# Layer-0 input transposes of a two-layer graph-attention and mixture-of-experts kernel: by a second, block-swapped load and VectorE in place of TensorE

## The chip, the cores and the metric

The kernel runs on one core of a Trainium2 chip. The metric is the device time of one execution in microseconds (us). The core has five engines with a queue of instructions each: TensorE (PE: matmuls and transposes; its weight loads are shown apart as PEld), VectorE (DVE), ScalarE (ACT), GpSimd (POOL) and SyncE (SP), which only issues transfers. An engine works through its queue in order; where an instruction needs another engine's result it waits, and all behind it wait too. Transfers run on 16 DMA engines.

## The reference, cut to what matters

64 batches of 256 rows with 256 columns, all float32, go through two layers. Each line below adds to its own input (a residual).

```python
x = x + elu(attention4(layernorm(x), adj, W0, a0))     # 4 heads of 64, masked softmax over 256 rows
x = x + layernorm(x) @ Wf.T + bf
x = x + relu(attention1(layernorm(x), adj, W1, a1))    # 1 head of 256
x = x + moe(layernorm(x))                              # router, the 2 best of 8 experts, gelu
```

The expert layer also adds its normalised input, as `moe` starts from its tokens. The change touches the first line only: there the kernel needs the projection `layernorm(x) @ W0` (with the score columns), and for TensorE the rows of x must lie transposed, columns on the partitions.

## The kernel before, in words

A batch is a tile of 128 partitions with two row tiles of 256 columns (`[P, NT, D]`). `load_batch` fetches it three batches ahead (`AHEAD`, six buffers). `batch_layers` (from line 370) is a generator that carries one batch through both layers. A hand-written schedule (from line 896) runs it: a step calls every active generator once, in the order of the ranks that they yield, and a new batch begins every third step (`TICKS`). So several batches are in work at a time, each some stages behind the next, and the order of instructions on every engine is fixed when the program is built. Routing work (`route`), done once per chunk of up to four batches, and the experts' work on pairs of 128 rows (`expert_pair`) are woven in by the same steps.

The stages that matter here:

- Line 375, `norm_stats(x0)`: VectorE takes mean and variance of the rows (lines 290 and 291), GpSimd turns the variance into 1/std, called `rstd` (lines 293 and 294). The mean is taken out through the weights, and `rstd` is applied after the projection, so the projection itself works on raw x.
- Line 376, `transposed(x0)`: four 128x128 transposes on TensorE into a PSUM bank (`pt`, line 301), and one ScalarE copy to SBUF (`xT`, line 305). The same helper is used three more times per batch, for x1, x2 and the normalised rows `xng`.
- Line 378, `projected`: the matmuls `pq<-wx,xT` of line 315, 268 wide in layer 0 and 259 in layer 1, then the exponentials on ScalarE (line 323) and the scaling on VectorE (line 327), which need `rstd`.
- `scores` (lines 339 and 346) and `attended` (matmuls `pv`, line 360; reciprocals, line 367), then hp, e, x1 (lines 388 to 398).
- The second transpose, the dense layer `pf` (line 408), then layer 1 in the same way, then router, sending of rows to the experts' regions (line 741), expert matmuls `ph` (649) and `py` (664), and scatters that add into the output (line 681), each of which waits for earlier ones.

SBUF tiles come from pools with a fixed number of buffers per name (`bufs`); a tile whose buffer is still being read makes its writer wait. `work` has two buffers unless a call says otherwise; `xT` has four, and they are shared by all the transposed tiles.

## Time and profile before

| | |
|---|---|
| time, median of 3 runs | 1795.14 us (1784.11 to 1803.95) |
| span of the profiled execution | 1821.2 us |
| mean granted TensorE clock | 0.937 of full |
| busy: PE, PEld, DVE, ACT, POOL | 89, 79, 68, 46, 60% of the span |
| DMA packets | 137,374, of them 18,680 under 512 B; 192.90 MB |
| DMA queue of SyncE (q1), of GpSimd (q0) | 22.0%, 20.6% of 16 engines |
| last layer-0 transpose starts at | 1450.2 us |

How to read the lines of a profile below. A group line gives the source line, the engine, the operation, the tiles it writes and reads (out<-in), their shapes and the number of instructions; behind the first bar the busy time in us and the mean length of one in ns; behind the second bar the idle time of the engine just before them, and what ended it. A timeline line gives the start in us, the length, and the same names; square brackets hold the idle time before it and its releaser. A line of busy time by stretch gives from:to, length, the busy time of PE, PEld, DVE, ACT and POOL with the number of instructions, then the granted clock, the DMA share and the GB/s. PE's matmuls are pipelined, so the distance from one start to the next says what a group costs the engine.

### The profile page before, as it was taken

What the parts mean: (1) busy time and instruction counts of PE and PEld (TensorE: products, weight loads), DVE (VectorE), ACT (ScalarE), POOL (GpSimd) and SP (SyncE); (2) the same over time, 40 slices, a digit from 0 to 9 for tenths busy, and PEclk for the clock granted to TensorE, in tenths of its full rate; (3) what the DMA queues carried; (4) which work ended last, traced back from release to release, by engine and by line L of the source; (5) the groups of instructions that cost most, each with busy time, mean ns of one, the idle gap of its engine ahead of it and who ended that gap; (6) DMA issues with size and microseconds to landing.
All of it is one profiled execution on the core that took longest, in us unless ns stands there. A gap on an engine that the chain in (4) does not pass through costs nothing. (4 is left out here: it accounts for less than half of the span.)

```text
span 1821.2 us, 30155 instructions
## 1 busy us (share of the span) xinstructions
PE 1629.5 (89%) x9254; PEld 1433.0 (79%) x9254; DVE 1231.4 (68%) x4680; ACT 839.9 (46%) x1773; POOL 1084.2 (60%) x1164
## 2 busy tenths in 40 slices
PE   6998889899999999999999999999989998778692
PEld 5787778788888888888878788887878887667582
DVE  6889887867685858686766768688678876522231
ACT  1243333355554555554545545555455545443241
POOL 1333645557575767767676757576685767644444
PEclk9999989899998999998989999999899989889897
DMA  4410211235344444544354534444353436576663
GB/s 137 140 36 24 71 60 53 79 109 121 105 95 104 109 126 108 132 103 110 93 119 112 119 91 95 118 111 128 84 127 101 107 82 166 118 186 139 135 139 43
DMA packets 137374, 192.90 MB, mean 106 GB/s; under 512 B 18680, under 2 KB 91392, under 8 KB 137216
## 3 DMA queue, kind: packets, MB, share of 16 engines
q1 hardware_dynamic: 86592, 122.61, 22.0%
q0 software_dynamic: 49632, 67.39, 20.6%
q8 instruction: 76, 1.25, 0.3%
q10 hardware_dynamic: 992, 0.99, 0.2%
q14 instruction: 82, 0.67, 0.1%
HBM read 101.77 MB, written 89.15 MB: 105 GB/s over the span
## 5 line engine op out<-in xcount | busy, mean ns | idle before, releaser
L681 POOL DMA_INDIRECT out_dram<-y,to x262 | 419.4, 1601 | 231.1 <-DMA out_dram<-y,to 103.5
L360 PE MATMUL pv<-q,z 128*128 128x65 f32 (+1 forms) x2560 | 394.4, 314 | 5.3 <-DVE z L346 5.0
L360 PEld LDWEIGHTS pv<-q,z 128*128 128x128 f32 x2560 | 364.9, 210 | 21.1 <-DVE z L346 5.4
L293 POOL TENSOR_SCALAR rstd<-mv 128x2 f32<-128x2 f32 x256 | 81.2, 317 | 376.2 <-DVE mv L291 355.6
L741 POOL DMA_INDIRECT xs<-xng,pos x248 | 261.2, 1053 | 68.2 <-issue 66.0
L315 PE MATMUL pq<-wx,xT 128*128 128x268 f32 (+1 forms) x1024 | 265.4, 402 | 35.8 <-ACT xT L305 31.8
L649 PE MATMUL ph<-sT,we 128*128 128x256 f32 x1048 | 252.6, 397 | 48.1 <-ACT sT L621 22.9
L346 DVE SCALAR_TENSOR_TENSOR z<-pd,q,mask 128x256 f32<-128x256 f32 x640 | 265.1, 473 | 9.9 <-PE pd L339 7.5
L649 PEld LDWEIGHTS ph<-sT,we 128*128 128x128 f32 x1048 | 205.0, 200 | 80.6 <-ACT sT L621 29.4
L664 PE MATMUL py<-w2s,hT 128*128 (+1 forms) x1176 | 265.4, 381 | 0.6 <-ACT hT L655 0.6
L315 PEld LDWEIGHTS pq<-wx,xT 128*128 128x128 f32 x1024 | 188.1, 194 | 85.8 <-ACT xT L305 50.6
L664 PEld LDWEIGHTS py<-w2s,hT 128*128 128x128 f32 x1176 | 220.5, 191 | 29.3 <-ACT hT L655 1.0
L305 ACT COPY xT<-pt 128x512 f32<-128x512 f32 x256 | 144.9, 589 | 192.8 <-PE pt L301 127.6
L327 DVE SCALAR_TENSOR_TENSOR q<-pq,rstd,q 128x256 f32<-128x256 f32 x256 | 112.4, 479 | 154.5 <-ACT q L323 150.7
L655 ACT ACTIVATE hT<-ph,we 128x256 f32<-128x256 f32 x294 | 123.3, 471 | 173.4 <-PE ph L649 122.9
L670 DVE TENSOR_TENSOR y<-py,b2s 128x512 f32<-128x512 f32 x147 | 96.7, 688 | 149.2 <-PE py L664 77.9
L294 POOL TENSOR_TENSOR rstd<-rstd,mhalf 128x2 f32<-128x2 f32 x256 | 184.2, 719 | 21.4
L642 ACT ACTIVATE y<-y,w 128x256 f32<-128x256 f32 x262 | 112.9, 498 | 177.5 <-DVE y L670 171.1
L290 DVE BATCH_NORM_STATS2 stats<-x 128x6 f32<-128x256 f32 x384 | 155.9, 406 | 0.0
L408 PE MATMUL pf<-wfT,xT 128*128 128x256 f32 x512 | 145.7, 435 | 0.1
L323 ACT ACTIVATE q<-pq,rstd 128x12 f32<-128x12 f32 (+1 forms) x256 | 56.5, 265 | 162.3 <-POOL rstd L294 150.8
L434 POOL TENSOR_TENSOR x<-x,rel 128x512 f32<-128x512 f32 x64 | 109.2, 1706 | 25.2 <-ACT rel L431 25.0
(147 smaller groups left out, 2259.2 us busy)
## 6 DMA issues: line engine op xcount, KB each, us to landing
we<-wpack SPq DMA_DIRECT2D x147, 288.0 KB
xr<-xs SPq DMA_DIRECT2D x131, 260.0 KB
xin<-in_x_dram SPq DMA_DIRECT2D x64, 256.0 KB
out_dram<-base SPq DMA_DIRECT2D x64, 256.0 KB
out_dram<-y,to POOLq DMA_INDIRECT x262
xs<-xng,pos POOLq DMA_INDIRECT x248
xs<-fill SPq DMA_DIRECT2D x9, 260.0 KB
wpack<-wt SPq DMA_DIRECT2D x8, 288.0 KB
```

The source lines that it names most:

```text
L290: nc.vector.bn_stats(stats[:, t, :], src[:, t, :])
L294: nc.gpsimd.tensor_tensor(rstd, rstd, mhalf, ALU.pow)
L305: nc.scalar.copy(dst, pt)
L315: nc.tensor.matmul(pq.rearrange("p h c -> p (h c)"), xT[:, k, t * P : (t + 1) * P], wx[:, k, :], start=(k == 0), stop=(k == KT - 1),)
L346: nc.vector.scalar_tensor_tensor(z[:, j, :], pd[:, i, :], q[:, j, h, d + 2 : d + 3], mask[:, j, :], op0=ALU.max, op1=ALU.mult,)
L360: nc.tensor.matmul(pv[:, h, :], z[:, j, t * P : (t + 1) * P], q[:, j, h, : d + 1], start=(j == 0), stop=(j == NT - 1),)
L408: nc.tensor.matmul(pf[:, t, :], xT[:, k, t * P : (t + 1) * P], wfT[:, k, :], start=(k == 0), stop=(k == KT - 1),)
L649: nc.tensor.matmul(ph[:, f, :], we[:, k * D + f * P : k * D + (f + 1) * P], xT[:, k, :], start=(k == 0), stop=(k == KT - 1),)
L655: nc.scalar.activation(hT[:, f, :], ph[:, f, :], AF.Gelu, bias=we[:, C_B1 + f : C_B1 + f + 1])
L664: nc.tensor.matmul(py[:, t, :], hT[:, f, t * P : (t + 1) * P], w2s[:, e, f * D : (f + 1) * D].rearrange("p e c -> p (e c)"), start=(f == 0 ...
L681: d = nc.gpsimd.indirect_dma_start(out=out_rows, out_offset=bass.IndirectOffsetOnAxis(ap=to[:, t : t + 1], axis=0), in_=y[:, t, :], in_off ...
L741: d = nc.gpsimd.indirect_dma_start(out=xs_d[: E * CAP * PAIR, :], out_offset=bass.IndirectOffsetOnAxis(ap=at, axis=0), in_=xe, in_offset=None,
```

## The change

The raw rows of a batch are loaded a second time, as `xblk`. Four transfers per batch, each for 32 partitions, place every 32x32 block of the batch where its transpose belongs; the runs are 32 floats long. VectorE's `transpose` then turns all the 32x32 blocks in place of their own, in one instruction of 128x512, which gives the whole transposed tile `xT`. TensorE's four transposes and ScalarE's copy for layer 0 are no longer there; the other three transposes of a batch stay as they were. The block tiles are loaded two batches ahead into three buffers. To make room in SBUF, the tiles e, x1b and rel go from two buffers to one. What it is for: to take work off TensorE.

```diff
+    def load_blocks(b):
+        t = io.tile([P, KT, N], F32, tag="xblk", name=f"xblk_{b}", bufs=3)
+        for g in range(P // S):
+            nc.sync.dma_start(
+                out=t[g * S : (g + 1) * S].rearrange("q k (c a) -> q k c a", a=S),
+                in_=x[b].rearrange("(c q) (k g a) -> g q k c a", q=S, g=P // S, a=S)[g],
+            )
+        return t
+
+    S = 32
+    AHEAD, BLOCKS_AHEAD = 3, 2
+    xblk = {0: load_blocks(0)}
     xin = {0: load_batch(0)}
...
+    xblk.update({b: load_blocks(b) for b in range(1, BLOCKS_AHEAD)})
     xin.update({b: load_batch(b) for b in range(1, AHEAD)})
...
         _, rstd = norm_stats(x0)
-        xT = transposed(x0)
+        xb = xblk.pop(b)
+        if b + BLOCKS_AHEAD < B:
+            xblk[b + BLOCKS_AHEAD] = load_blocks(b + BLOCKS_AHEAD)
+        xT = work.tile([P, KT, N], F32, tag="xT", name="xT", bufs=4)
+        nc.vector.transpose(xT.rearrange("p k n -> p (k n)"), xb.rearrange("p k n -> p (k n)"))
         yield 20
...
-        ex = work.tile([P, NT, D], F32, tag="e", name="e")
+        ex = work.tile([P, NT, D], F32, tag="e", name="e", bufs=1)
...
-        x1b = work.tile([P, NT, D], F32, tag="x1b", name="x1b")
+        x1b = work.tile([P, NT, D], F32, tag="x1b", name="x1b", bufs=1)
...
-        rel = work.tile([P, NT, D], F32, tag="rel", name="rel")
+        rel = work.tile([P, NT, D], F32, tag="rel", name="rel", bufs=1)
```

## The prediction

> **What bounds the kernel now.** I read the page's first part, the groups by shape, the waits, the busy time by stretch, and the timeline of two batches.

> ```profile
> PE 1629.5 (89%) x9254; PEld 1433.0 (79%) x9254; DVE 1231.4 (68%) x4680; ACT 839.9 (46%) x1773; POOL 1084.2 (60%) x1164
> ```

> TensorE (PE) is the bound. By stretch (us; then busy time of PE, PE's weight loads, VectorE, ScalarE, GpSimd; clock; DMA share; GB/s):

> ```profile
> 60.00:300.00 240.00, 217.86 (x1304) 189.76 (x1303) 199.59 (x690) 84.45 (x200) 107.41 (x156) 0.94 0.18 57
> 300.00:900.00 600.00, 569.75 (x3355) 505.90 (x3354) 435.46 (x1619) 313.32 (x652) 399.91 (x433) 0.96 0.43 107
> ```

> PE is 91 to 95% busy, but VectorE (DVE) is 83% busy before 300 us and 73% after: it has room in sum, not everywhere. The groups of the work that moves, and the nearest DVE row:

> ```profile
> L305 ACT COPY xT<-pt 128x512 f32<-128x512 f32 x256 | 144.9, 589 | 192.8 <-PE pt L301 127.6 <-PE pl L475 42.4 <-remote 12.2
> ...
> L397 DVE SCALAR_TENSOR_TENSOR x<-hp,xin 128x512 f32<-128x512 f32 x64 | 43.9, 685 | 0.0
> ...
> L301 PE MATMUL pt<-ident,xin 128*128 128x128 f32 x256 | 39.8, 280 | 0.0
> ```

> A share says nothing about order, so the deciding view is the timeline (start, length, engine, line). One early batch:

> ```profile
> 112.25 0.60 PE L301 MATMUL pt<-ident,xin 128*128 128x128 f32 x4
> ...
> 112.69 0.38 PE L339 MATMUL pd<-ident,q 128*128 128x128 f32 x2
> ...
> 113.63 2.07 PE L315 MATMUL pq<-wx,xT 128*128 128x268 f32 x8 [0.56 <-ACT xT L305]
> ...
> 115.36 0.18 DVE L291 BATCH_NORM_AGGREGATE mv<-stats 128x2 f32<-128x6 f32 x1
> 115.46 0.85 DVE L346 SCALAR_TENSOR_TENSOR z<-pd,q,mask 128x256 f32<-128x256 f32 x2
> ...
> 115.98 3.68 PE L360 MATMUL pv<-q,z 128*128 128x65 f32 x32
> ...
> 119.70 0.18 DVE L367 RECIPROCAL rinv<-pv 128x4 f32<-128x4 f32 x1 [1.60 <-PE pv L360]
> ```

> PE runs the layer-0 projection (pq, 268 wide) at 113.63, while DVE finishes the statistics of the same rows only at 115.5. DVE runs about 2 us behind PE here, and nobody minds, because the projection needs xT and not the statistics.

> What an idle PE costs beyond the idle time shows at 1044 us:

> ```profile
> 1044.43 1.09 PE L617 MATMUL px<-ident,xr 128*128 128x128 f32 x4 [2.53 <-DMA xr<-xs]
> 1045.31 6.93 PE L360 MATMUL pv<-q,z 128*128 128x65 f32 x32
> 1052.04 3.00 PE L408 MATMUL pf<-wfT,xT 128*128 128x256 f32 x8
> ```

> After a gap of 2.53 us the same 32 matmuls take 6.93 us and not 3.68, and the next eight 3.00 and not 1.95 (their usual length in this stage): 4.3 us more. Shorter gaps, such as the 0.56 above, are followed by normal lengths.

> [...]

> **The change, part by part.**

> Removed from PE: four transposes of xin per batch. By start to start (112.25 to 112.69) they take 0.44 us, so 64 x 0.44 = 28 us. The 0.56 wait for ScalarE's copy goes too. Removed from ScalarE: 64 copies x 0.589 = 38 us, at 46% busy and off the path: worth nothing by itself.

> Added to DVE: 64 transposes of 128x512 f32. Below: as fast as the 685 ns row of that size. [...] I take 0.75 with its start, 48 us in sum. That DVE has room for.

> Moved: who makes xT. In the changed program's instruction order the transpose stands on DVE right behind the statistics of the same rows, and the projection on PE, unmoved in PE's order, now waits for DVE. This is the step that decides. In the batch above DVE could begin at 115.46 and end at 116.2. PE, without its four transposes and the copy's wait, is there at 113.07 - 0.44 = 112.6. A gap of 3.6 us takes the place of one of 0.56, and the projection starts 2.6 us later than before. Queued behind it on PE are xng's transposes, the experts' transposes px and the 32 attention matmuls (pv); for those DVE's rinv already waits (1.60). So DVE's next round starts later as well, it has hardly a gap from 119.70 to the next statistics, and the delay isn't caught up. The gap is also over 2.5 us, so the slow clock is due: up to 4.3 more. That is 6.9 us for a plain early batch of 15.7. Where routing work lies on DVE (batches 9, 10, 13, 14, 17, 18) the lag in the trace is 5 to 11 us, but the second of each pair has part of it paid by the first, and present PE waits (3.41 us for x at 163.5) fall away. I take 5.5 as the mean over the 19 batches before 350 us: 105 us.

> From there on, with two experts per batch on PE, the lag repeats in groups of four batches, about 100 us. One of the four, in the timeline:

> ```profile
> 1017.72 1.97 PE L315 MATMUL pq<-wx,xT 128*128 128x268 f32 x8
> ...
> 1020.76 0.18 DVE L291 BATCH_NORM_AGGREGATE mv<-stats 128x2 f32<-128x6 f32 x1
> ```

> With 0.75 us behind the statistics, xT would come, against the present start of the projection: 1.5 us early (the batch at 972 us), 1.0 late (995), 4.0 late (the one shown), 2.6 late (1038). With the 0.44 saved, gaps of 0, 1.4, 4.4 and about 2. The 4.4 costs the slow clock as well, 4.3. Given back: the wait for xr near 1041 to 1044 (3.1 in three pieces), whose own slow stretch now belongs to the gap before it, and 4 x 0.44 = 1.8. So 1.4 + 4.4 + 4.3 + 2 - 3.1 - 1.8 = 7. DVE's own waits in the group (2.65 and 4.94 us for ScalarE's q) take up some: I take 4 per group, 11 groups, 44 us.

> Added DMA: 64 x 4 transfers, each 512 runs of 128 B: 131,072 packets beside 137,374, 16.8 MB beside 193. Price per packet: below 14 ns (down from the 18 of 256 B), above 74 ns, the mean of queue q1 (22.0% of 16 x 1821.2 us over 86,592). At 16 ns it is 131 us per engine, 7% of the span on top of 43%: hidden, as a batch's blocks are asked for two batches ahead (30 us or more) and take some 2 us (10 at the upper price). Issue: a 512-run weight load costs SyncE 0.62 us, so 2.5 us per batch, in a queue that stands waiting 545 us for sent rows alone (its waits). At the start the first block load goes ahead of xin and the weights: +2 us.

> Cut buffers (e, x1b, rel from two to one): in the early batches x1b is read by 106.7 and rewritten at 113.1, e read by 110.8 and rewritten at 120.6, rel longer still. Nothing.

> Tail after the last projection (1454 us): same work, but the scatters, which wait 103.5 us on one another, get more time before it: -10.

> Sum: 105 + 44 + 2 - 10 = +141 us, with the 28 already taken off inside: 1795 + 141 = 1936.

> **Rivals.**
> *Waits without the clock (1850).* Gaps stay below what drops the clock, or DVE, freed by PE's pauses, catches up. Then only net delays remain: about 2.6 in half of the early batches (25) and 2 to 3 per group (30): +55. For it: DVE's idle 27% after 300 us. Against: DVE waits on PE's pv 91 times, so it cannot run ahead.
> *Hidden (1767, the other side).* xT is ready in time and the 28 us are pure gain. For it: PE at 95%, ScalarE relieved, one batch in four with xT early. Against: the statistics ahead of the transpose end after the projection's present start in three of four.
> *Packets (2065).* At 74 ns, DMA goes from 43 to 76%; the scatter chain (103.5 us of waits) and xr loads stretch by about 130 on top of 1936. Against: 18 ns for 256 B.

> **How the numbers follow.** Chances: 0.60 for 1936, 0.20 for 1850, 0.10 for 1767, 0.10 for 2065. The range leaves out the last two and takes in 1850 with 20 below it[...]: 1830 to 2010. Faster by over 1% 0.10; within 1% 0.04, from the low end of the second case; slower 0.86.

> **What would show it.** Right: projection matmuls waiting on the DVE transpose, some 100 to 200 us in over 40 waits; pv matmuls of double length behind them; a lower granted clock, most before 350 us; PE's busy share down; no DVE wait for xblk. Wrong: pq without idle, or DVE waiting for xblk, or scatters with longer landings. What would break the forecast most: a clock that doesn't drop, or a transpose far from 0.75 us.

## The result, and the profile after

| | before | changed |
|---|---|---|
| time, median | 1797.05 us (4 runs, 1784.11 to 1803.95) | 1928.24 us (4 runs, 1926.26 to 1936.97) |
| ratio to before | | 1.0748, 95% interval 1.0679 to 1.0818 |
| mean granted TensorE clock, profiled execution | 0.937 | 0.928 |

The changed kernel is 131 us slower, where 141 was forecast (1936), and the time lies in the range. One caution for all that follows: single executions of the kernel before spread over some 25 us, and its profiled one (span 1821.2) lies at the slow end, so the text compares spacings of batches and medians, not the two spans.

The same views as before, in the same order. The page's first part:

```profile
PE 1595.1 (83%) x8998; PEld 1397.3 (73%) x8998; DVE 1278.9 (66%) x4744; ACT 809.3 (42%) x1709; POOL 1081.5 (56%) x1164
```

TensorE has 256 transposes fewer (8998 instructions instead of 9254), and its share fell from 89 to 83%: it is busy for 34 us less (1595.1, 1629.5 before) while the time grew by 131, so it idles more than it saves. VectorE has 64 instructions more, 47.5 us, and its share fell too. So neither engine is held by the amount of its own work; something makes both wait. By stretch (PE, PEld, DVE, ACT, POOL, then clock, DMA share, GB/s):

```profile
60.00:300.00 240.00, 174.68 (x1005) 150.58 (x1004) 167.62 (x545) 61.09 (x144) 77.86 (x117) 0.87 0.26 66
300.00:900.00 600.00, 518.21 (x3070) 458.40 (x3069) 436.46 (x1584) 274.37 (x574) 365.70 (x408) 0.95 0.44 106
```

Before 300 us TensorE did 1005 matmuls where the kernel before did 1304, and its clock fell from 0.94 to 0.87. Who made it wait is in the chief group of the projection and in the list of waits (us in total, times, longest):

```profile
L329 PE MATMUL pq<-wx,xT 128*128 128x268 f32 (+1 forms) x1024 | 311.7, 455 | 220.5 <-DVE xT L394 197.8
```

```profile
PE pq L329 <- DVE xT L394: 197.8, 53, 11.9
```

The idle time ahead of the projections was 35.8 us before, nearly all of it for ScalarE's copy. It is 220.5 now, and 197.8 of that is waiting for VectorE's transpose, in 53 of 64 batches. The mean length grew from 402 to 455 ns as well, all of it in layer 0: the 128x268 matmuls go from 411 to 516 ns, the 128x259 ones stay at 394. Of the 512 in layer 0, 198 ran at a granted clock of 0.50, 667 ns each on the mean, against 407 for the 281 at full clock; in the kernel before 26 ran at 0.50. The transposed tile itself:

```profile
L105 SPq DMA_DIRECT2D xblk<-in_x_dram x256: 578/623/1748, 0.8 to 1504.6; - x128
L394 DVE STREAM_TRANSPOSE xT<-xblk x64: 692/711/714, 13.5 to 1559.2; 128x512 f32<-128x512 f32 x64
its engine sat idle before it (us, times) until:
who waited for it (us, times):
  PE pq L329: 197.8, 53
```

A transpose takes 711 ns, and VectorE never sat idle ahead of one: the list under "until" is empty. So the blocks were there each time, and no transfer stands behind the wait. VectorE was still busy with what its order puts first. An early batch shows it:

```profile
130.60 0.41 PE L353 MATMUL pd<-ident,q 128*128 128x128 f32 x2
...
133.71 0.18 DVE L305 BATCH_NORM_AGGREGATE mv<-stats 128x2 f32<-128x6 f32 x1
...
133.89 0.71 DVE L394 STREAM_TRANSPOSE xT<-xblk 128x512 f32<-128x512 f32 x1
...
134.65 2.07 PE L329 MATMUL pq<-wx,xT 128*128 128x268 f32 x8 [3.64 <-DVE xT L394]
...
137.00 3.68 PE L374 MATMUL pv<-q,z 128*128 128x65 f32 x32
...
140.72 0.18 DVE L381 RECIPROCAL rinv<-pv 128x4 f32<-128x4 f32 x1 [1.60 <-PE pv L374]
```

VectorE works without a break through the statistics of other batches' rows, then of these, then turns the blocks. TensorE stands for 3.64 us, and then VectorE stands 1.60 us for TensorE's pv, just as before: neither can get ahead of the other. Later, TensorE's own rows in one group of four batches:

```profile
1011.90 0.38 PE L353 MATMUL pd<-ident,q 128*128 128x128 f32 x2
1016.46 3.62 PE L329 MATMUL pq<-wx,xT 128*128 128x268 f32 x8 [4.18 <-DVE xT L394]
...
1020.93 3.69 PE L374 MATMUL pv<-q,z 128*128 128x65 f32 x32
...
1036.33 0.38 PE L353 MATMUL pd<-ident,q 128*128 128x128 f32 x2
1038.89 2.07 PE L329 MATMUL pq<-wx,xT 128*128 128x268 f32 x8 [2.18 <-DVE xT L394]
...
1041.24 1.48 PE L635 MATMUL px<-ident,xr 128*128 128x128 f32 x12
```

After the gap of 4.18 us the eight projection matmuls take 3.62 us and not 2.07, and pv behind them runs at full speed again. After 2.18 us nothing is slow. The wait of px for xr that the kernel before had here is gone: the gaps ahead of the projections have paid for it.

### The profile page after: what moved, and what is told of

Same layout as the page of the kernel before. It is cut to its first block, busy times and chain, and to the rows that moved or that the text cites. A ratio compares the mean times of both kernels' runs of the same rounds, so it can differ in the third digit from the quotient of the medians.

```text
span 1926.7 us, 29984 instructions
## 1 busy us (share of the span) xinstructions
PE 1595.1 (83%) x8998; PEld 1397.3 (73%) x8998; DVE 1278.9 (66%) x4744; ACT 809.3 (42%) x1709; POOL 1081.5 (56%) x1164
## 5 line engine op out<-in xcount | busy, mean ns | idle before, releaser
L329 PE MATMUL pq<-wx,xT 128*128 128x268 f32 (+1 forms) x1024 | 311.7, 455 | 220.5 <-DVE xT L394 197.8
L329 PEld LDWEIGHTS pq<-wx,xT 128*128 128x128 f32 x1024 | 213.0, 219 | 285.8 <-DVE xT L394 194.4
L374 PE MATMUL pv<-q,z 128*128 128x65 f32 (+1 forms) x2560 | 363.9, 298 | 0.0
L374 PEld LDWEIGHTS pv<-q,z 128*128 128x128 f32 x2560 | 337.8, 196 | 13.9
L667 PE MATMUL ph<-sT,we 128*128 128x256 f32 x1048 | 250.3, 395 | 43.9 <-ACT sT L639 24.0
L360 DVE SCALAR_TENSOR_TENSOR z<-pd,q,mask 128x256 f32<-128x256 f32 x640 | 264.6, 471 | 10.1 <-PE pd L353 10.1
L319 ACT COPY xT<-pt 128x512 f32<-128x512 f32 x192 | 112.3, 585 | 182.5 <-PE pt L315 181.4
L381 DVE RECIPROCAL rinv<-pv 128x4 f32<-128x4 f32 (+1 forms) x256 | 40.2, 170 | 193.9 <-PE pv L374 193.7
L412 ACT ACTIVATE e<-hp 128x512 f32<-128x512 f32 x64 | 40.3, 630 | 218.1 <-DVE hp L406 218.1
```

What stands on the lines that cost most here:

```text
L329: nc.tensor.matmul(pq.rearrange("p h c -> p (h c)"), xT[:, k, t * P : (t + 1) * P], wx[:, k, :], start=(k == 0), stop=(k == KT - 1),)
L360: nc.vector.scalar_tensor_tensor(z[:, j, :], pd[:, i, :], q[:, j, h, d + 2 : d + 3], mask[:, j, :], op0=ALU.max, op1=ALU.mult,)
L374: nc.tensor.matmul(pv[:, h, :], z[:, j, t * P : (t + 1) * P], q[:, j, h, : d + 1], start=(j == 0), stop=(j == NT - 1),)
L667: nc.tensor.matmul(ph[:, f, :], we[:, k * D + f * P : k * D + (f + 1) * P], xT[:, k, :], start=(k == 0), stop=(k == KT - 1),)
```

## The experiments

The theory is that the place of the transpose in VectorE's order costs the time. Rivals are the transfers and their packets, VectorE's extra work as such, the cut buffers, and a clock that falls by itself. Spacings below are from one start of a layer-0 projection to the next.

### Both made: all of the change but who makes xT

```diff
-        xT = work.tile([P, KT, N], F32, tag="xT", name="xT", bufs=4)
-        nc.vector.transpose(xT.rearrange("p k n -> p (k n)"), xb.rearrange("p k n -> p (k n)"))
+        turned = work.tile([P, KT, N], F32, tag="turned", name="turned", bufs=1)
+        nc.vector.transpose(turned.rearrange("p k n -> p (k n)"), xb.rearrange("p k n -> p (k n)"))
+        xT = transposed(x0)
```

> The changed kernel, with its block loads, its VectorE transposes and its cut buffers, but the transposes go into a tile that nobody reads, and TensorE and ScalarE make xT as before. If the loss is the wait of the projection for VectorE: near the kernel before, 1797 to 1815 us (the start still loads more). If it is VectorE's added load, the small packets or the cut buffers: 1920 to 1950, as in the changed kernel or above it.

Measured: 1796.65 us, ratio 1.0028 (1.0007 to 1.0049). The loads, the small packets, 64 more VectorE instructions in the very same place and the cut buffers cost together 0.3%, some 5 us (0.07 to 0.5% by the interval). The early stretch is as it was, with a DMA share of 0.32 where the kernel before had 0.18:

```profile
60.00:300.00 240.00, 217.42 (x1314) 189.66 (x1313) 210.38 (x708) 85.22 (x202) 108.66 (x157) 0.94 0.32 80
```

So it isn't the work that VectorE was given. It is that somebody waits for it.

### Copy on VectorE: only the lag, with nothing else of the change

The kernel before, with the copy of layer 0's transposes out of PSUM made by VectorE instead of ScalarE. TensorE still transposes; there are no block loads.

```diff
-        xT = transposed(x0)
+        xT = transposed(x0, copy=nc.vector.tensor_copy)
```

> The kernel before, and only the copy of the layer-0 transposes out of PSUM goes from ScalarE to VectorE, right behind the statistics: no block loads, no cut buffers, TensorE's transposes stay. If the wait for VectorE's place in the order is the cause: about as slow as the changed kernel, 1890 to 1960 us. If packets or buffers are: 1797 to 1810.

Measured: 1929.06 us, ratio 1.0748 (1.0712 to 1.0785): as much as the whole change, from handing one copy per batch to another engine. The waits:

```profile
PE pq L315 <- DVE xT L305: 177.1, 55, 12.2
```

TensorE keeps its 28 us of transposes here, but it does them where it would otherwise stand idle: the gap of a plain early batch is 3.10 us and not 3.65. Together the two runs show the cause from both sides: everything except the dependence costs 0.3%, and the dependence alone costs as much as the change.

### Ahead of the statistics: the same transpose, four instructions earlier

```diff
-        _, rstd = norm_stats(x0)
...
         nc.vector.transpose(xT.rearrange("p k n -> p (k n)"), xb.rearrange("p k n -> p (k n)"))
+        _, rstd = norm_stats(x0)
```

> The changed kernel, with the VectorE transpose ahead of the statistics of the same rows and not behind them, some 1.1 us earlier on VectorE. If the lag of VectorE is the cause, each of the 53 waits shrinks by about 1.1 us and the time falls by 50 to 60, to 1865 to 1885 us. If load, packets or buffers are: no change, 1920 to 1935.

Measured: 1865.9 us, ratio 1.0418 (1.0373 to 1.0463), 62 us less than the change. Each kind of gap shrank by 1.05 us (3.65 to 2.60, 4.18 to 3.13, 2.18 to 1.13, 1.17 to 0.12), about what the two pairs of statistics last (133.89 less 132.75 = 1.14 in the early batch above). The waits fell by 52.8 us in total; the other 9 were not measured apart, and the granted clock rose from 0.928 to 0.934.

```profile
PE pq L329 <- DVE xT L393: 145.0, 42, 10.8
```

What is left of the wait is the work of other batches that still stands ahead on VectorE.

### A batch earlier: the lag taken away

VectorE turns the blocks of the next batch while this one starts, behind its statistics, so each transpose has a whole batch of time. The transposed tile has two buffers of its own, and the shared xT three instead of four.

```diff
+        if b == 0:
+            turn(0)
         _, rstd = norm_stats(x0)
+        if b + 1 < B:
+            turn(b + 1)
+        xT = xT0.pop(b)
```

> The changed kernel, with the VectorE transpose of batch b + 1 issued at the start of batch b, so one batch earlier, into a tile of its own with two buffers (the shared xT goes from four to three). Work and transfers are the same. If the lag is the cause: the waits are gone, and what was taken off TensorE shows: 1765 to 1795 us. If load, packets or buffers are: 1910 to 1935.

Measured: 1803.8 us, ratio 1.004 (1.0018 to 1.0062). The wait for VectorE's transpose is gone from the list, and with it the loss. But 28 us of TensorE work are gone too, and of those nothing shows in the time. A miss, and the most useful one. Early on something does show: from the second projection to the 20th it is 314.8 us, where the kernel before took 324.7. But the second projection starts 9.7 us later (34.45 against 24.71), which takes it all back. Later the chief wait is another:

```profile
PE px L645 <- DMA xr<-xs: 29.3, 30, 2.7
```

In the timeline of a group of four:

```profile
447.49 0.63 PE L645 MATMUL px<-ident,xr 128*128 128x128 f32 x4 [2.09 <-DMA xr<-xs]
449.21 2.23 PE L645 MATMUL px<-ident,xr 128*128 128x128 f32 x8 [1.09 <-DMA xr<-xs]
451.23 6.93 PE L374 MATMUL pv<-q,z 128*128 128x65 f32 x32
457.95 3.72 PE L436 MATMUL pf<-wfT,xT 128*128 128x256 f32 x8
```

TensorE comes sooner to px, and the experts' rows aren't there yet. Behind these waits of 2.09 and 1.09 us pv takes 6.93 us and not 3.68, and pf 3.72 and not 1.95.

### Fill the wait: the clock's share by itself

The changed kernel with 28 transposes that nobody reads in the gap ahead of the projection, in the first 20 batches and in the one batch of each later four that has the 4.2 us gap: 31 in all. They are extra work, and keep TensorE busy for some 3 us (an estimate: 28 quarters of the 0.44 us of four transposes in the kernel before).

```diff
+        if b < 20 or b % 4 == 2:
+            idle = bank("idle", [P])
+            for _ in range(28):
+                nc.tensor.transpose(idle, x0[:, 0, :P], ident)
         q = projected(xT, wx0, H, rstd)
```

> The changed kernel, with 28 extra 128x128 transposes on TensorE, into a bank that nobody reads, right ahead of the projection in the batches that wait longest (the first 20, and of each later four the one that waits 4.2 us). They take 3.1 us of a wait that is there anyway. If the slow clock behind a wait costs 1 to 2 us each time, as the changed kernel's trace has it: 30 waits, so 1890 to 1905 us. If it costs nothing: 1925 to 1935. If it cost the 4.3 us of the prediction: 1830 to 1860.

Measured: 1903.11 us, ratio 1.0559 (1.0492 to 1.0626): 25 us less than the change by the medians, 34 by the two ratios to before (0.0189 of 1797), so 0.8 to 1.1 per filled gap and not 4.3. The early clock is whole again, and the mean of the profiled execution is 0.951, as in the kernel before on the same chip (0.936 to 0.951):

```profile
60.00:300.00 240.00, 206.33 (x1384) 183.65 (x1384) 178.75 (x589) 64.28 (x153) 85.61 (x126) 0.95 0.28 72
```

The spacing of the plain batches (us, from batch 4 to batch 8) splits the early loss cleanly:

| | spacing, mean of four | more than before |
|---|---|---|
| before, and "both made" | 15.4 | |
| changed, wait filled | 18.2 | 2.8 |
| changed | 20.0 | 4.6 |

So a plain early batch loses 2.8 us by waiting and 1.8 by the clock. The price per gap is a net one. In the six early batches with routing work gaps of 3.7 to 8.9 us remain. And in five of the later groups the slow stretch has moved to the next gap, the one of 2.18 us that cost nothing at 1038.89 above. The same batch here:

```profile
1017.64 3.76 PE L329 MATMUL pq<-wx,xT 128*128 128x268 f32 x8 [2.18 <-DVE xT L394]
```

### Three attempts to collect the 28 us, and what they met

*A mended start.* "A batch earlier", with the first three batches transposed by TensorE and the block loads behind the weights.

```diff
-    xblk = {0: load_blocks(0)}
+    FIRST = 3
+    xblk = {}
...
+        xT = xT0.pop(b) if b >= FIRST else transposed(x0)
```

> The kernel with the transpose a batch earlier, but the first three batches are transposed by TensorE as before, and the first block loads are issued behind the weights. If the block loads at the front are what puts its first projection 9 us late: 1792 to 1798 us, 6 to 10 below it and level with the kernel before. If not: 1800 to 1806.

Measured: 1814.25 us, ratio 1.0063 (1.0037 to 1.009). A miss; the two intervals overlap, so the mended start is neither shown better nor worse. The second projection starts at 31.3 us instead of 34.4, but the kernel before has it at 24.7: the block loads at the front are only about 3 of those 10 us. The traces show a second cause in the start. The tile e, cut to one buffer, is also the one into which the attention vectors of both layers are loaded when the weights are prepared (wx_a). The two loads in the kernel before (first and last start at the end of the line), then in the mended start, and VectorE's wait there:

```profile
L154 ACTq DMA_DIRECT2D wx_a<-in_L_gnn_a_dram x2: 453/488/522, 1.3 to 1.9; - x2
...
L168 ACTq DMA_DIRECT2D wx_a<-in_L_gnn_a_dram x2: 341/428/516, 1.3 to 11.7; - x2
...
  DMA wx_a<-in_L_gnn_a_dram: 3.2, 1
```

With one buffer layer 1's load waits until layer 0's vectors have been read. It starts at 11.7 us and not at 1.9 (15.5 in the changed kernel), and VectorE stands 3.2 us for it. How much of the late start it makes was not measured apart. Further on, more groups fall into the wait for xr with a slow stretch behind it (pv takes over 4.5 us in 7 batches between 350 and 1190 us, against 5 in the trace of "a batch earlier"), such as this one:

```profile
1031.26 0.63 PE L646 MATMUL px<-ident,xr 128*128 128x128 f32 x4 [2.26 <-DMA xr<-xs]
...
1034.82 6.93 PE L374 MATMUL pv<-q,z 128*128 128x65 f32 x32
```

*Pairs two steps later.* The mended start, and also the kernel before, with the experts' pairs begun two steps later, so that their rows have more time.

```diff
         if n:
+            if not last:
+                yield 95
+                yield 95
             regs = {}
```

> The same with the start mended, and expert pairs of a chunk become due two steps after its rows are sent (not for the last chunk), so that TensorE does not reach a pair's transposes before its rows are in. If the work taken off TensorE is lost in that wait and the slow clock behind it: 1740 to 1775 us. If it isn't: 1790 to 1805, or more by what is moved into the tail.

> The kernel before with the pairs two steps later and nothing else, the control of the one above. If the wait for a pair's rows costs this kernel its 3 us and the slow clock in each group of four batches: 1750 to 1780 us, and above the other by up to 28, what TensorE is spared. If not: 1795 to 1810.

Measured: 1899.1 us (ratio 1.053, 1.046 to 1.06) and 1879.34 us (1.038, 1.0279 to 1.0481). Both lie 124 and 99 us above the range of the theory, and above the rival's figures too. In the second, 30 us are lost by the last projection (1484.2 us, 1454.0 in the profiled execution of before, itself a long one), and 22 more from there to the end (388.9, 367.2). TensorE has new waits for VectorE, and the wait for xr has only shrunk, from 25.4 us:

```profile
PE pv L360 <- DVE y L670: 22.8, 13, 2.1
PE pt L301 <- DVE z L346: 18.3, 10, 2.1
PE px L617 <- DMA xr<-xs: 16.7, 14, 3.0
```

Two steps move whole stages of the pairs against everything else, into new waits and into the tail, where the wait asked for 3 us. What share each has was not measured apart.

*One rank later, not two steps.* The last attempt moves px only behind the attention matmuls pv of the same step, 3.7 us of work, by one rank, once on "a batch earlier" and once on the kernel before.

```diff
-        yield 40
+        yield 55
         px = bank("px", [KT, PAIR])
```

> The block transpose a batch earlier, as in the run of that name, and the experts' transposes px placed behind the layer-0 attention matmuls pv of the same step, not ahead of them. Theory (the 28 us saved on TensorE turned into a wait of px for the loaded rows xr, and the wait into slow matmuls): pv fills the wait, px waits under 0.5 us per group of four, no pv of double length at 450 or 645 us, 1755 to 1785. Rival (something else than xr holds the rate, such as VectorE): the waits move to pv or to the projections, 1795 to 1815.

> The kernel before, with px behind pv in the same way. Theory: its wait for xr of 2 to 3 us per group and the slow stretch behind it go too, 1765 to 1785, about 15 above the other run, as the 28 us on TensorE can then show in part. Rival: no better than before, 1790 to 1810, and no difference between the two runs.

Measured: 1764.87 us (ratio 0.9844, 0.9773 to 0.9915) and 1763.09 us (0.9834, 0.9763 to 0.9904). Both beat the kernels before and after, though the second was expected some 15 us above the first. The wait for xr fell to 3.6 us in the first and 7.7 in the second, and pv takes its 3.7 us in every batch from 350 to 1190 us. But the two are equal, so the 28 us still don't show. One part is the start again: the first kernel's second projection comes 9.75 us later (34.80 against 25.05), and by the 21st it has only about made that up (370.2 against 369.1). For the rest, the same place in both timelines tells why. First "a batch earlier" with px later:

```profile
627.01 3.69 PE L374 MATMUL pv<-q,z 128*128 128x65 f32 x32
630.53 1.48 PE L645 MATMUL px<-ident,xr 128*128 128x128 f32 x12
634.35 3.35 PE L436 MATMUL pf<-wfT,xT 128*128 128x256 f32 x8 [2.34 <-DVE q L341]
637.50 0.97 PE L353 MATMUL pd<-ident,q 128*128 128x128 f32 x4
```

and the kernel before with px later:

```profile
626.31 3.68 PE L360 MATMUL pv<-q,z 128*128 128x65 f32 x32
629.83 1.48 PE L617 MATMUL px<-ident,xr 128*128 128x128 f32 x12
632.82 1.99 PE L408 MATMUL pf<-wfT,xT 128*128 128x256 f32 x8 [1.51 <-DVE q L327]
634.65 0.60 PE L339 MATMUL pd<-ident,q 128*128 128x128 f32 x4
```

The wait is for q, and it goes back past VectorE, which stands idle itself. In the first kernel:

```profile
633.51 0.43 ACT L337 ACTIVATE q<-pq,rstd 128x12 f32<-128x12 f32 x2 [3.86 <-POOL rstd L308]
633.81 0.88 DVE L341 SCALAR_TENSOR_TENSOR q<-pq,rstd,q 128x256 f32<-128x256 f32 x2 [4.33 <-ACT q L337]
```

and in the second:

```profile
631.97 0.43 ACT L323 ACTIVATE q<-pq,rstd 128x12 f32<-128x12 f32 x2 [4.46 <-POOL rstd L294]
632.28 0.88 DVE L327 SCALAR_TENSOR_TENSOR q<-pq,rstd,q 128x256 f32<-128x256 f32 x2 [4.93 <-ACT q L323]
```

VectorE waits for ScalarE, and ScalarE for GpSimd's rstd. GpSimd goes through the same series of work in both, from the first sending of rows (xs) to that rstd in 13.5 us. TensorE, with less to do, reaches pv 0.83 us sooner in that series, and so waits that much longer: the gap grows from 1.51 to 2.34 us. With that the matmuls behind it slow down, and pf and pd take 1.7 us more. That is 2.5 us against the 1.76 saved by four batches without transposes. Between 350 and 1190 us the granted clock falls seven times, for 3.41 us each, in the first kernel and not once in the second. The spacing of a group agrees: 94.59 us with the change, 94.08 without (mean of seven groups, batches 24 to 52). The mended start together with the later px was not run.

## Why the prediction was right, and which terms were off

**The step that decides** (xT comes from VectorE, behind the statistics of the same rows, and the unmoved projection waits): right, and shown. The gap of a plain early batch was to be 3.6 us and is 3.65; those of a group of four were to be 0, 1.4, 4.4 and about 2, and are 0, 1.17, 4.18 and 2.18; the waits were to be 100 to 200 us in over 40, and are 197.8 in 53. In the six batches with routing they are 6.74 to 11.87 us; VectorE's place in the trace of before, with 0.75 us added, gives 6.8 to 12.0 for the same batches. All of it comes from comparing where VectorE stood with where TensorE needed the result. One discount failed: the second of each pair was to have part of its lag paid by the first, but its gap is the longer one each time (10.62 after 8.65, 11.51 after 9.66, 11.87 after 6.74).

**The net wait per early batch**, 2.6 us: 2.8 with the clock filled in.

**The slow clock**, "up to 4.3 more" behind each long gap: mis-sized. It is 1.8 us in a plain early batch, 1.6 after the 4.18 us gap at 1016, 0.8 to 1.1 on the mean of the 31 filled gaps. The pv of double length did not come; up to the last projection none takes over 4.5 us. The 4.3 was read off one stretch of before, behind a broken-up wait for xr, and the price doesn't follow from the length of a gap. The granted clock in the trace shows what it follows from (stretch, its length, busy time of the five engines, clock; the last line is that stretch of before):

```profile
129.36:132.77 3.41, 1.65 (x11) 1.24 (x9) 3.34 (x12) 3.22 (x8) 2.49 (x2) 1.00 0.00 0
132.78:136.18 3.40, 1.53 (x7) 1.31 (x8) 2.51 (x8) 0.84 (x3) 1.85 (x5) 1.00 0.52 153
1013.41:1016.81 3.40, 0.35 (x2) 0.32 (x3) 3.26 (x11) 0.00 (x0) 3.10 (x4) 1.00 0.54 76
1016.83:1020.23 3.40, 3.40 (x10) 2.50 (x9) 1.53 (x4) 1.71 (x4) 3.23 (x6) 0.50 0.23 33
...
1043.94:1054.16 10.22, 9.73 (x41) 9.40 (x42) 3.99 (x19) 3.37 (x8) 4.70 (x5) 0.50 0.62 150
```

**5.5 us over 19 batches, 105 us**: measured by the 20th projection, 90 us against the trace of before and 83 against that of "both made", start included. The mean is 4.4 to 4.7; from the second projection on, so without the start, it is 77 and 80 us, 4.3 to 4.5 each. A plain batch lost 4.6 and not 6.9: the smaller clock term.

**4 us per group of four, 44 us**: the total of 131 less 83 to 90 leaves 41 to 48 for everything after. But its size hangs on how the kernel before ran: against "both made", whose groups last 94.23 us, the changed kernel's 99.53 are 5.3 more; against the profiled execution of before (99.13) only 0.4. The kernel before presumably has the wait for xr and its slow stretch in some executions more than in others; only one of them was traced. That it was "given back" is right; how much stays open.

**Start, +2**: too small. The second projection starts 12.7 us later than before, and 9.6 later already in "both made". The block load of batch 0 goes ahead of the weights, worth about 3 us by the mended start, and the cut buffer of e holds back a weight load, as shown there. Not all of it is left at the end, as "both made" as a whole costs 5 us. **Tail, -10**: from the last projection to the end it is 366.8 us, and 367.2 before. Nothing was gained.

**Transpose 0.75 us**, an estimate of the author's beside the 685 ns row of that size: 711 ns (median; 692 to 714). (That row is another operation, a scalar_tensor_tensor.) The 2010 at the upper end of the range was an estimate too. **Packets at 16 ns**, hidden: the 128 B packets take 13.8 ns on the mean, where the 1,024 of 256 B in the kernel before took 18.0; that is 113 us per DMA engine, and in "both made" everything but the dependence, the packets with it, costs 0.3%. **Cut buffers, nothing**: right for the batches by the same run, but wrong for the start. The prediction looked for readers of e, x1b and rel in the batches only, and e serves the weights as well.

**Waits against clock.** That the total came so near is in part luck: two terms were off in opposite directions. The rival without the clock put 55 us on the waits, which leaves 86 of the forecast's 141 to the clock. With the long gaps filled the kernel still loses some 100 us (ratio 1.0559), so the waits, with the start, cost about 100 and the clock 25 to 34. The waits are larger since every early batch has one, where the rival counted half, since the batches with routing have gaps of 7 to 12 us, to which it gave 2.6 like the others, and since the start costs more and the tail gives nothing back. So the waits were the larger part, as that rival had it, but larger than it said, and the clock is not nothing.

**The other rivals.** "Packets" is out. "Hidden" is out too, and one thing no case held: even without the lag its 1767 doesn't come. The saved 28 us go into the later start and into a wait for the next thing in line, first xr, then GpSimd's rstd by way of q.

## What to carry to other kernels

Before you move work to an engine with room, look up in the timeline where that engine stands when the result is needed: here VectorE ran about 2 us behind, and a transpose of 0.71 us on it left TensorE standing for 3.65 us in a plain early batch. Then ask what else is due just behind the work that is taken off the busiest engine: of 28 us nothing showed in "a batch earlier" (ratio 1.004), with 29.3 us of waits for xr behind it; take the wait that shows up next as the new question. Here the cheapest gain was no saved work at all, but one rank (ratio 0.9834): px, which waits for a transfer, put behind 3.7 us of pv matmuls that are ready.

## What the runs showed of the hardware that was not expected

- The length of a gap alone doesn't tell what the clock then costs; in the trace of the changed kernel the clock fell 42 times, each time behind a stretch between two points 3.41 us apart with 2.0 us or more idle in it. The same gap of 2.18 us ahead of the same projection cost nothing in the changed kernel (2.07 us at 1038.89), where such a point at 1037.30 cuts it into 0.59 and 1.59, and 1.7 us with the wait filled (3.76 at 1017.64), where the whole gap lies between two such points (1014.36 and 1017.78). After px waits of 2.09 and 1.09 us (at 447) pv and pf lost some 5 (6.93 and 3.72 us, where 3.68 and 1.95 are usual).
- 131,072 packets of 128 B, almost as many as all others together, took 13.8 ns each, and a block load of 64 KB in 512 runs landed in 4.2 us (median; 2.3 to 6.4). The kernel's time moved by 0.3%, with everything else in "both made".
- With px behind pv the time also spreads less: 1760.45 to 1766.54 us over 4 runs, where the kernel before on the same chip had 1782.65 to 1802.46 over 6. That fits a wait whose slow stretch comes in some executions and not in others; it isn't shown.
